# Rows copied one by one on two queues instead of one, and basis products chunk by chunk, in a two-layer relational graph kernel

## The chip, the cores and the metric

The kernel runs on one core of one Trainium2 chip. The metric is device time in microseconds, from the first to the last instruction and what lies around them, for one execution; lower is better. The engines of the core are named as in the profile: PE (matrix products, with PEld for its weight loads), DVE (vector), ACT (scalar), POOL (GpSimd), and SP or SyncE, which computes nothing and issues DMAs. SPq and ACTq mark the instruction queues of SyncE and ACT when they issue DMAs.

## The reference

Two layers of a relational graph convolution over 50,000 nodes of 128 features, a residual, and a layer norm. The edge list holds 800,000 edges and 50,000 self loops, sorted by destination; each edge has one of 16 relations, and the weight of a relation is a mix of 8 basis matrices.

```python
def _rgcn_layer(h, src, dst, rel, basis, w_comp, loop_w, bias):
    W = jnp.einsum('rb,bio->rio', w_comp, basis)
    seg = dst.astype(jnp.int32) * N_REL + rel.astype(jnp.int32)
    agg = jax.ops.segment_sum(h[src], seg, num_segments=N_ENT * N_REL)
    agg = agg.reshape(N_ENT, N_REL, -1)
    msg = jnp.einsum('nri,rio->no', agg, W)
    out = msg + h @ loop_w + bias
    return jax.nn.relu(out)

h = _rgcn_layer(entity_emb, src, dst, rel_type, basis1, w_comp1, loop_w1, bias1)
h = _rgcn_layer(h, src, dst, rel_type, basis2, w_comp2, loop_w2, bias2)

x = _layernorm(x + h, axis=-1)
```

## The kernel before

The edges that are not self loops are cut into tiles of 128 edges (P) and chunks of 10 tiles (K). There are 625 chunks (C), and each of the two layers goes through all of them, so the main loop (L978) makes 1,250 turns. The first turns of the first layer also sort the edge list into its tables (`runs`, `rows_of`), in steps between the other work.

For one chunk the following happens.

- The source rows of its tiles are brought in. A tile is usually one gather on POOL: `gather` (L206) takes 128 indices from `src` and fetches 128 rows of 512 bytes into one of five buffers `g` (GATHERS). The gathers of chunk c + 2 are issued at the start of chunk c (L985 to L988).
- In every eighth chunk the last tile is not gathered. `row_by_row` (L839) copies it: SyncE loads the 128 byte offsets of the tile from DRAM (`row_at`, L842), then, 32 at a time, into its registers (L851, a TENSOR_LOAD in the profile, four for a tile), and for each row issues one DMA of 512 bytes whose source address comes from a register (L859, a MOVE and a DMA_DIRECT2D in the profile). `by_hand` (L835) says which chunks have such a tile: 15, 23, ... 623, which are 77 tiles in a layer. The copy begins BY_HAND + EARLY = 11 chunks ahead of its use and is spread over 8 chunks, one step after each tile of the main loop (L1032).
- DVE builds the weighted one-hot matrix `hot` of a later chunk (`hot_of`, L904), from relation weights that PE makes for four chunks at a time (`weights`, L621). These need the table `rel`, which SyncE loads (L625), and the comparison `is_rel` on DVE (L632).
- PE multiplies each tile's rows by `hot` into the bank `pa` (L1016), five tiles to a bank, and ACT evicts the bank into `aT` (L1024). There are two banks `pa`.
- The sums of four chunks (BATCH) stand side by side in one `aT`, 480 columns. `slots_of_batch` (L750) multiplies them by the 8 basis matrices, 8 products over 480 columns (L754), has ACT copy the result to `by_slot` (L760), transposes it back in four pieces on PE (L764), and `spread_out` (L738) spreads each piece over the places of its nodes on DVE (`slots`, L742). The last five chunks of a layer use `slots` (L728) instead: 8 products of 128 columns for one chunk (L732), whose result needs no transposing.
- `to_nodes` (L785) adds the slots of a chunk into the sums of its group of 512 nodes (`pn`, L796), six chunks behind (LAG). `from_itself` (L681) makes the part of the self loops for a group: it loads `h_own` (L685) and, for every fourth group, the table `lrel` (L652), transposes, and multiplies by the bases (L710, L717, L725). `finish` (L813) closes a group: it adds both parts (L817), and in the first layer applies relu and stores `H1` (L821), in the second adds `x` (`xw`, loaded at L795), normalizes (`normed`) and stores the result (L826).

The order of the work on PE, POOL, DVE and ACT is the order of the program text: `beside` (L952) hands out the steps of the side work between two tiles of the main loop, and the whole loop stands under a manual schedule of these four engines (L898). SyncE isn't in that list; its instructions are placed by the tile framework. Each engine runs its instructions in order, and a DMA that waits for a semaphore holds what is queued behind it. The DMAs that SyncE and ACT issue take their completion semaphores in turn from the same eight (101 to 105 and 107 to 109 in the trace, where ten DMAs of ACT at the start and all of SyncE's use them), and each waits for the DMA that used the semaphore before it.

Of the kernel before, what the change touches and what calls it, by code (L numbers as in the profile page):

```python
# [72 lines left out]
BATCH = 4  # L73
BY_HAND = 8
EARLY = 3
OFFSETS = 32
LAG = BATCH + 2
# [8 lines left out]
def tile_rgcn_resnorm(  # L86
# [33 lines left out]
    assert D == P and N >= P and edges.shape[0] == 1 and AT * NR == P and PER * NB * WN <= BANK and AT * PER * NB == WEIGHTS and PER == HALF and S <= P and C >= 4 and M > 0 and N % C == 0 and N % J == 0 and J * D == BANK and C % BATCH == 1 and C > 4 * BATCH and RUN - LK // 2 == LIVE and C <= RUN and 2 * C <= NG * P and N <= 1 << 16 and E % ROW == 0  # L120
# [10 lines left out]
    ROW_AT = dram.tile([2 * C, P], I32, name="ROW_AT")  # L131
# [310 lines left out]
    def rows_of(j, pool):  # L442
# [36 lines left out]
        row_at = pool.tile([P, LIVE], F32, name="real").bitcast(I32)[:, :P]  # L479
        nc.vector.tensor_scalar(row_at[:m], srcf[:m, LIVE - P :], float(N - 1), float(4 * D), op0=OP.min, op1=OP.mult)  # L480
        nc.sync.dma_start(ROW_AT[r0 : r0 + m], row_at[:m])
# [63 lines left out]
    def count_up(pool):  # L545
        last = 5 * NG + len(ROWS)
        off = pool.tile([P, RUN], F32, name="k_f")[0:1, :C]
        even = pool.tile([P, RUN], F32, name="loop_f")[0:1, :C]
# [48 lines left out]
    def chunked():  # L597
        with (
# [7 lines left out]

            ALONE = C - BATCH - 1

# [12 lines left out]
            def weights(c, n):  # L621
# [9 lines left out]
                is_rel = hp.tile([P, LIVE], F32, name="is_rel", bufs=1)  # L631
# [14 lines left out]
            def loop_weights(g, n):  # L646
# [14 lines left out]
                is_rel = rel.bitcast(F32)  # L661
                for h in range(2):
                    nc.vector.tensor_scalar(is_rel[:m, h, :], rel[:m, h, :], its_rel1[:m], None, op0=OP.is_equal)
                    if h == 0:
                        yield
                po = ps_o.tile([P, BANK], F32, name="po")
                of = po[:, : J * T * NB].rearrange("p (j t) -> p j t", j=J)
                for j in range(J):
                    for h in range(2):
                        nc.tensor.matmul(  # L670
                            of[:, j, :],
                            is_rel[:m, h, :].rearrange("k (p j) -> k p j", j=J)[:, :, j],
                            EACH[n][:m, :T, :].rearrange("k t b -> k (t b)"),
                            start=h == 0,
                            stop=h == 1,
                        )
# [4 lines left out]
            def from_itself(g, of, n):  # L681

                m = nodes(g)
                h = sb.tile([P, J, D], F32, name="h_own", bufs=1)
# [43 lines left out]
            def slots(c, k, aT, n):  # L728

                ps = ps_s.tile([P, BANK], F32, name="ps")  # L730
                for b in range(NB):
                    nc.tensor.matmul(  # L732
                        ps[: k * WN, :D], aT[:, b, : k * WN], BASIS[n][:, b, :], start=b == 0, stop=b == NB - 1
                    )
                    yield
                yield spread_out(c, ps[:, :D])

            def spread_out(c, of):  # L738

                k = ks(c) * WN  # L740
                st = sb.tile([P, J, D], F32, name="slots", bufs=BATCH)
                nc.vector.tensor_tensor(  # L742
                    st[:k],
                    of[:k, None, :].to_broadcast([k, J, D]),
                    which[:k, c, :, None].to_broadcast([k, J, D]),
                    op=OP.mult,
                )
                return st

            def slots_of_batch(c, aT, st, n):  # L750

                ps = ps_s.tile([P, BANK], F32, name="ps")
                for b in range(NB):
                    nc.tensor.matmul(  # L754
                        ps[:, : BATCH * S], BASIS[n][:, b, :], aT[:, b, :], start=b == 0, stop=b == NB - 1
                    )
                    if b < NB - 1:
                        yield
                by_slot = sb.tile([P, BATCH * S], F32, name="by_slot", bufs=1)
                nc.scalar.copy(by_slot, ps[:, : BATCH * S])  # L760
                yield
                po = ps_o.tile([P, BANK], F32, name="po")
                for q in range(BATCH):
                    nc.tensor.transpose(po[:S, q * P : (q + 1) * P], by_slot[:, q * S : (q + 1) * S], ident)  # L764
                    if q == 1:
                        yield
                for q in range(BATCH):
                    st[c + q] = spread_out(c + q, po[:, q * P : (q + 1) * P])
                    if q == 1:
                        yield  # L770
                yield
# [61 lines left out]
            behind = []  # L833

            def by_hand(c):  # L835

                return ks(c) == K and c >= BY_HAND + EARLY and c % BY_HAND == BY_HAND - 1

            def row_by_row(c, of):  # L839

                row_at = hp.tile([1, P], I32, name="row_at")
                nc.sync.dma_start(row_at, ROW_AT[2 * c + 1 : 2 * c + 2])  # L842
                to = hp.tile([P, D], F32, name="by_hand")
                byte = of.bitcast(U8).rearrange("n d -> (n d)")
                yield to
                steps = BY_HAND * (K - 1)
                for step in range(steps):
                    for e in range(step * P // steps, (step + 1) * P // steps):
                        if e % OFFSETS == 0:
                            with tc.issue_after(behind[-1]) if behind else ExitStack():  # L850
                                _, offsets = nc.values_load_multi_w_load_instructions(  # L851
                                    row_at[:, e : e + OFFSETS],
                                    engines=[mybir.EngineType.SP],
# [5 lines left out]
                        behind[:] = [nc.sync.dma_start(row, byte[None, ds(offsets[e % OFFSETS], 4 * D)]).ins]  # L859
# [39 lines left out]
            for n, of in enumerate((x, H1)):  # L899
# [21 lines left out]
                def sum_up(c):  # L921
                    at = c % BATCH * S
                    for st[c] in slots(c, ks(c), aTs[c // BATCH][:, :, at : at + S], n):
                        yield

                def added_in(c):

                    if c < ALONE + 2:
                        return [c - LAG] if c >= LAG else []
                    at = ALONE - BATCH + 2 * (c - ALONE - 2)  # L930
                    return [at, at + 1] if c < C else list(range(at, C))

                def own_of_all():

                    for g in range(NGR):
                        while now[0] < min(first(g) + LAG - 5, C - LAG - 2):
# [9 lines left out]
                def add(c):  # L946

                    for g in to_nodes(c, n):
                        assert made[0] > g
                        ending.append(finish(g, n))  # L950

                def beside(t, c, owning, summing):  # L952
# [3 lines left out]
                    if c < ALONE + 2:  # L956
                        if t in (1, 3, 6, 9):
                            next(summing, None)
                    elif 1 <= t <= 4:
                        for _ in range(NB // 4):  # L960
                            next(summing, None)
                        if t == 4:
                            done(summing)
                            if c == C - 1:
                                done(sum_up(c - 1))
# [3 lines left out]
                    if t == 8:  # L969
                        for one in added_in(c):  # L970
                            add(one)
# [4 lines left out]
                handed, fetching = {}, iter(())  # L976
                owning = own_of_all()
                for c in range(C):  # L978
                    now[0] = c
                    if n == 0 and c:  # L980

                        next(coming, None)
                        while ready[0] + 1 < len(ROWS) and 2 * min(C, c + FETCH + 5 + BY_HAND + EARLY) > ROWS[ready[0] + 1]:
                            next(coming)
                    for to in range(0 if c == 0 else c + FETCH, min(C, c + FETCH + 1)):  # L985
                        buffer = (n * C + to) % GATHERS
                        for k in range(ks(to) - by_hand(to)):
                            gather(rows[buffer][:, k, :], of, src[:, to * K + k : to * K + k + 1])  # L988
                    to = c + BY_HAND + EARLY
                    if to < C and by_hand(to):  # L990
                        fetching = row_by_row(to, of)
                        handed[to] = next(fetching)
                    g = rows[(n * C + c) % GATHERS]
# [7 lines left out]
                    if c % BATCH == 0:  # L1001
                        aTs[c // BATCH] = hp.tile([P, NB, BATCH * S], F32, name="aT")
                    aT, place_of = aTs[c // BATCH], c % BATCH * S
                    if c >= ALONE + 2:
                        if c == ALONE + 2:
                            done(summing)
                        summing = sum_up(c - 2)
                    elif c % BATCH == 0:
                        summing = slots_of_batch(c - BATCH, aTs[c // BATCH - 1], st, n) if c else iter(())
                    for k in range(0, K, PER):  # L1010
# [3 lines left out]
                        for i in range(PER):  # L1014
                            if i < m:
                                nc.tensor.matmul(  # L1016
                                    pa[:, i * NB * WN : (i + 1) * NB * WN],
                                    g[:, k + i, :] if k + i < ks(c) - by_hand(c) else handed.pop(c),
# [4 lines left out]
                            if i == m - 1:  # L1023
                                nc.scalar.copy(  # L1024
                                    aT[:, :, place_of + k * WN : place_of + (k + m) * WN].rearrange(
                                        "d b (i w) -> d i b w", w=WN
                                    ),
# [3 lines left out]
                            if k + i < K - 1:  # L1031
                                next(fetching, None)  # L1032
# [7 lines left out]
                    for one in added_in(c + 1) if c + 1 < C else ():  # L1040
                        masks[one] = masks_of(one)
# [6 lines left out]
                for one in added_in(C):  # L1048
                    masks[one] = masks_of(one)
                    if one == C - 1:  # L1050
                        done(sum_up(one))
                    add(one)
                for each in ending:
# [192 lines left out]
```

## Time and profile before

| what | value |
|---|---|
| median of 3 runs | 18,807.65 us (18,802.19 to 18,828.18) |
| the profiled execution | 18,802.19 us |
| its span, first to last instruction | 18,800.3 us |
| busy: PE / DVE / ACT / POOL | 62% / 36% / 10% / 62% |
| gathers on POOL | 12,346, of 0.946 to 0.949 us each |
| rows copied by SyncE | 19,712, in 154 tiles |
| register loads for them | 616 |
| ACT evictions into aT | 2,500 of 558 ns |
| ACT copies by_slot | 310 of 559 ns |
| mean granted TensorE clock | 0.758 |

A chunk takes 18,800.3 / 1250 = 15.04 us on average. Busy times of the table leave out what an engine spends on issuing DMAs, on registers and on semaphores, so SyncE does not appear in it; its queue is read from the timeline and from the list of what SyncE waits for. "Remote" in a list of waits is a release for which the profile shows no instruction, and "issue" is time in which nothing that the profile shows was waited for.

### The profile page before, as it was taken

The numbers are of one execution on the slowest core, as the hardware profiler recorded it, in microseconds if no ns is written. First come the engines' busy times: TensorE is split into PE (matmuls) and PEld (weight loads), VectorE is DVE, ScalarE is ACT, GpSimd is POOL, SyncE is SP. The second block draws the span as 40 slices with busy tenths as digits, with TensorE's granted clock in tenths as the row PEclk, the third lists the DMA queues.
The fourth block names the chain that finished last, engine by engine and source line by source line (L and its number), as shares of the span: only waits on it lengthen the run. The fifth ranks groups of instructions, "written<-read, shape, count | busy, mean of one in ns | idle before, by whom it ended". The sixth has DMA issues, their size and how long they took to land. (4 is left out here: it accounts for less than half of the span.)

```text
span 18800.3 us, 177030 instructions
## 1 busy us (share of the span) xinstructions
PE 11698.6 (62%) x45072; PEld 7678.2 (41%) x45072; DVE 6710.9 (36%) x11506; ACT 1919.7 (10%) x3706; POOL 11722.7 (62%) x12379
## 2 busy tenths in 40 slices
PE   4565555656566666666656666666666666666666
PEld 3343333434344444444434444444444444444444
DVE  4343434434333333333333333333333333333333
ACT  0000000101000000000001111111111111111111
POOL 5656555665666666666656666666666666666665
PEclk8777777777777777777777777777777777777778
DMA  2222222222111111211112222222222222222221
GB/s 64 62 58 60 56 55 57 58 61 58 54 54 53 53 53 53 54 53 53 53 48 56 56 55 56 56 56 56 56 56 56 56 55 56 56 56 56 56 56 52
DMA packets 576545, 1047.67 MB, mean 56 GB/s; under 512 B 232236, under 2 KB 297674, under 8 KB 575518
## 3 DMA queue, kind: packets, MB, share of 16 engines
q0 software_dynamic: 398624, 816.71, 16.7%
q1 hardware_dynamic: 173678, 218.10, 3.6%
q8 instruction: 366, 6.00, 0.1%
q14 instruction: 661, 5.41, 0.1%
q10 hardware_dynamic: 3216, 1.45, 0.0%
HBM read 962.38 MB, written 72.95 MB: 55 GB/s over the span
## 5 line engine op out<-in xcount | busy, mean ns | idle before, releaser
L206 POOL DMA_INDIRECT g<-H,src x6173 | 5841.2, 946 | 3351.6 <-issue 1363.6
L206 POOL DMA_INDIRECT g<-in_x_dram,src x6173 | 5855.6, 949 | 3273.2 <-issue 1384.3
L1016 PEld LDWEIGHTS pa<-hot,g 128*128 128x128 f32 x24692 | 4644.3, 238 | 5656.9 <-issue 4927.7
L1016 PE MATMUL pa<-hot,g 128*128 128x96 f32 x24692 | 4690.0, 317 | 2628.5 <-issue 2005.6
L754 PE MATMUL ps<-aT,basis 128*128 128x480 f32 x4960 | 2970.5, 684 | 805.0 <-issue 426.6
L1024 ACT COPY aT<-pa 128x480 f32<-128x480 f32 x2500 | 1386.5, 558 | 15442.9 <-remote 8515.6
L796 PE MATMUL pn<-slots,own 120*128 120x512 f32 x4128 | 2523.9, 734 | 665.6 <-DVE slots L742 239.9
L710 PE MATMUL po<-basis,hT 128*128 128x512 f32 x3136 | 2093.6, 756 | 1140.6 <-DVE by L717 774.2
L717 DVE TENSOR_TENSOR by<-po,lw 128x512 f32<-128x512 f32 x1568 | 1066.9, 686 | 4103.6 <-remote 1913.1
L913 DVE TENSOR_TENSOR hot<-fixed,own 128x960 f32<-128x960 f32 x1250 | 1446.5, 1157 | 1582.5 <-remote 708.5
L725 DVE TENSOR_REDUCE ls<-by 128x128 f32<-128x1152 f32 (+1 forms) x784 | 1662.8, 2121 | 35.3 <-DVE by L717 0.9
L742 DVE TENSOR_TENSOR slots<-po,which 120x512 f32<-120x512 f32 x1240 | 780.9, 680 | 2377.2 <-remote 1013.7
L796 PEld LDWEIGHTS pn<-slots,own 120*128 120x128 f32 x4128 | 855.8, 235 | 1237.3 <-issue 729.3
L764 PE MATMUL po<-ident,by_slot 128*120 128x128 f32 x1240 | 374.8, 402 | 1413.2 <-ACT by_slot L760 867.6
L754 PEld LDWEIGHTS ps<-aT,basis 128*128 128x128 f32 x4960 | 898.3, 225 | 862.0 <-issue 471.2
L710 PEld LDWEIGHTS po<-basis,hT 128*128 128x128 f32 x3136 | 578.2, 230 | 1221.6 <-DVE by L717 821.7
L906 DVE TENSOR_TENSOR own<-fixed,key 128x120 bf16<-128x120 f32 x1250 | 343.1, 274 | 1997.9 <-remote 1037.8
L764 PEld LDWEIGHTS po<-ident,by_slot 128*120 128x120 f32 x1240 | 206.0, 208 | 1465.0 <-ACT by_slot L760 911.5
L779 DVE TENSOR_SCALAR own<-col,node 120x128 f32<-120x128 f32 x2064 | 533.7, 297 | 10.4 <-PE pn L796 10.4
L632 DVE TENSOR_SCALAR is_rel<-rel,its_rel 128x640 f32<-128x640 uint8 x314 | 178.5, 568 | 913.8 <-DMA rel<-REL 755.4
L637 PE MATMUL fixed<-each,is_rel 128*128 128x64 f32 x3140 | 445.1, 295 | 6.0 <-DVE is_rel L632 5.7
L637 PEld LDWEIGHTS fixed<-each,is_rel 128*128 128x128 f32 x3140 | 431.7, 216 | 7.1 <-DVE is_rel L632 6.9
(140 smaller groups left out, 3096.2 us busy)
## 6 DMA issues: line engine op xcount, KB each, us to landing
by_hand<-in_x_dram SPq DMA_DIRECT2D x9856, 0.5 KB
by_hand<-H SPq DMA_DIRECT2D x9856, 0.5 KB
g<-in_x_dram,src POOLq DMA_INDIRECT x6173
g<-H,src POOLq DMA_INDIRECT x6173
rel<-REL SPq DMA_DIRECT2D x312, 80.0 KB
h_own<-in_x_dram SPq DMA_DIRECT2D x97, 256.0 KB
xw<-in_x_dram SPq DMA_DIRECT2D x97, 256.0 KB
H<-ls SPq DMA_DIRECT2D x97, 256.0 KB
```

Of the source, the lines that this page charges most:

```text
L206: return nc.gpsimd.indirect_dma_start(out=to, out_offset=None, in_=of, in_offset=bass.IndirectOffsetOnAxis(ap=idx, axis=0))
L637: nc.tensor.matmul(of[:, :, j * NB : (j + 1) * NB], is_rel[:m, j * P : (j + 1) * P], EACH[n][:m], start=True, stop=True,)
L710: nc.tensor.matmul(hb[:m], hT[:, j, :m], BASIS[n][:, b : b + few, :].rearrange("p b d -> p (b d)"), start=True, stop=True,)
L717: nc.vector.tensor_tensor(by[:m, b : b + few, :], hb[:m].rearrange("p (b d) -> p b d", d=D), lw[:m, j, g % T, b : b + few, None].to_broadc ...
L725: nc.vector.tensor_reduce(ls[:m, j, :], by[:m].rearrange("p b d -> p d b"), AX.X, OP.add)
L742: nc.vector.tensor_tensor(st[:k], of[:k, None, :].to_broadcast([k, J, D]), which[:k, c, :, None].to_broadcast([k, J, D]), op=OP.mult,)
L754: nc.tensor.matmul(ps[:, : BATCH * S], BASIS[n][:, b, :], aT[:, b, :], start=b == 0, stop=b == NB - 1)
L764: nc.tensor.transpose(po[:S, q * P : (q + 1) * P], by_slot[:, q * S : (q + 1) * S], ident)
L796: nc.tensor.matmul(sums[g], own, of[:k].rearrange("s j d -> s (j d)"), start=c == first(g), stop=c == final(g),)
L913: nc.vector.tensor_tensor(hot[:, : ks(c)], pm[:, c % Q * K : c % Q * K + ks(c), :, None].to_broadcast([P, ks(c), NB, WN]), own[:, : ks(c), ...
L1016: nc.tensor.matmul(pa[:, i * NB * WN : (i + 1) * NB * WN], g[:, k + i, :] if k + i < ks(c) - by_hand(c) else handed.pop(c), hot[:, k + i]. ...
L1024: nc.scalar.copy(aT[:, :, place_of + k * WN : place_of + (k + m) * WN].rearrange("d b (i w) -> d i b w", w=WN), pa[:, : m * NB * WN].rearr ...
```

## The change

- The basis products are made for each chunk. `slots_of_batch` and `spread_out` go; `slots` serves all chunks, two chunks behind, and DVE spreads its result from the bank `ps` directly. The copy `by_slot` on ACT and the four transposes go too. A chunk is added to its nodes three chunks behind instead of six.
- Two engines copy rows. HANDS names them: SyncE takes the last free tile of the chunks c > 5 with c % 5 = 4 (9, 14, ... 624), ACT that of the chunks c > 6 with c % 6 = 2 (8, 14, ... 620). These are 124 and 103 tiles in a layer. Where a chunk has both, SyncE takes the last tile and ACT the one before it. ROW_AT holds two tiles of offsets for a row of edges instead of one; the offsets of both engines are loaded by SyncE. A copy begins one chunk more than its period ahead of use (6 and 7 chunks), and is spread over 5 and 6 chunks.
- Some buffers become separate or more: `is_l` for the compared `lrel`, two each for `h_own` and `is_rel`, three `aT` of one chunk.

```diff
-BATCH = 4
-BY_HAND = 8
-EARLY = 3
+SP_EVERY = 5
+ACT_EVERY = 6
...
-    ROW_AT = dram.tile([2 * C, P], I32, name="ROW_AT")
+    ROW_AT = dram.tile([2 * C, 2, P], I32, name="ROW_AT")
...
-                is_rel = hp.tile([P, LIVE], F32, name="is_rel", bufs=1)
+                is_rel = hp.tile([P, LIVE], F32, name="is_rel")
...
-                is_rel = rel.bitcast(F32)
+                is_rel = hp.tile([P // 2, 2, P, J], F32, name="is_l", bufs=1)
...
-                h = sb.tile([P, J, D], F32, name="h_own", bufs=1)
+                h = sb.tile([P, J, D], F32, name="h_own", bufs=2)
...
-                yield spread_out(c, ps[:, :D])
-
-            def spread_out(c, of):
-
-                k = ks(c) * WN
-                st = sb.tile([P, J, D], F32, name="slots", bufs=BATCH)
+                st = sb.tile([P, J, D], F32, name="slots")
                 nc.vector.tensor_tensor(
-                    st[:k],
-                    of[:k, None, :].to_broadcast([k, J, D]),
-                    which[:k, c, :, None].to_broadcast([k, J, D]),
+                    st[: k * WN],
+                    ps[: k * WN, None, :D].to_broadcast([k * WN, J, D]),
+                    which[: k * WN, c, :, None].to_broadcast([k * WN, J, D]),
                     op=OP.mult,
                 )
-                return st
-
-            def slots_of_batch(c, aT, st, n):
-
-                ps = ps_s.tile([P, BANK], F32, name="ps")
-                for b in range(NB):
-                    nc.tensor.matmul(
-                        ps[:, : BATCH * S], BASIS[n][:, b, :], aT[:, b, :], start=b == 0, stop=b == NB - 1
-                    )
...
-                by_slot = sb.tile([P, BATCH * S], F32, name="by_slot", bufs=1)
-                nc.scalar.copy(by_slot, ps[:, : BATCH * S])
...
-                    nc.tensor.transpose(po[:S, q * P : (q + 1) * P], by_slot[:, q * S : (q + 1) * S], ident)
...
+                yield st
...
-            behind = []
+            behind = {}
+            HANDS = ((nc.sync, SP_EVERY, SP_EVERY - 1), (nc.scalar, ACT_EVERY, ACT_EVERY // 2 - 1))

             def by_hand(c):

-                return ks(c) == K and c >= BY_HAND + EARLY and c % BY_HAND == BY_HAND - 1
-
-            def row_by_row(c, of):
-
-                row_at = hp.tile([1, P], I32, name="row_at")
-                nc.sync.dma_start(row_at, ROW_AT[2 * c + 1 : 2 * c + 2])
-                to = hp.tile([P, D], F32, name="by_hand")
+                if ks(c) < K:
+                    return []
+                return [i for i, (_, every, at) in enumerate(HANDS) if c > every and c % every == at]
+
+            def row_by_row(i, c, of):
+
+                engine, every, _ = HANDS[i]
+                tile_at = 1 - by_hand(c).index(i)
+                row_at = hp.tile([1, P], I32, name=f"row_at{i}", bufs=2)
+                nc.sync.dma_start(row_at, ROW_AT[2 * c + 1 : 2 * c + 2, tile_at])
+                to = hp.tile([P, D], F32, name=f"by_hand{i}", bufs=2)
                 byte = of.bitcast(U8).rearrange("n d -> (n d)")
                 yield to
-                steps = BY_HAND * (K - 1)
+                steps = every * (K - 1)
                 for step in range(steps):
                     for e in range(step * P // steps, (step + 1) * P // steps):
                         if e % OFFSETS == 0:
-                            with tc.issue_after(behind[-1]) if behind else ExitStack():
+                            with tc.issue_after(behind[i]) if i in behind else ExitStack():
                                 _, offsets = nc.values_load_multi_w_load_instructions(
                                     row_at[:, e : e + OFFSETS],
-                                    engines=[mybir.EngineType.SP],
+                                    engines=[engine.engine],
...
-                        behind[:] = [nc.sync.dma_start(row, byte[None, ds(offsets[e % OFFSETS], 4 * D)]).ins]
+                        behind[i] = engine.dma_start(row, byte[None, ds(offsets[e % OFFSETS], 4 * D)]).ins
                     yield to
...
-                        for k in range(ks(to) - by_hand(to)):
+                        for k in range(ks(to) - len(by_hand(to))):
                             gather(rows[buffer][:, k, :], of, src[:, to * K + k : to * K + k + 1])
-                    to = c + BY_HAND + EARLY
-                    if to < C and by_hand(to):
-                        fetching = row_by_row(to, of)
-                        handed[to] = next(fetching)
+                    for i, (_, every, _) in enumerate(HANDS):
+                        to = c + every + 1
+                        if to < C and i in by_hand(to):
+                            fetching[i] = row_by_row(i, to, of)
+                            handed.setdefault(to, {})[K - 1 - by_hand(to).index(i)] = next(fetching[i])
...
-                    elif c % BATCH == 0:
-                        summing = slots_of_batch(c - BATCH, aTs[c // BATCH - 1], st, n) if c else iter(())
+                    aT = aTs[c] = hp.tile([P, NB, S], F32, name="aT", bufs=3)
+                    summing = sum_up(c - 2) if c > 1 else iter(())
```

## The prediction, made before the changed kernel was run

> **What bounds the kernel now.** I first read the page: which engine is fullest, and what it does. Then the list of waits, the SyncE queue's own waits, and the timelines of the SyncE queue and of POOL, side by side.
>
> ```profile
> PE 11698.6 (62%) x45072; PEld 7678.2 (41%) x45072; DVE 6710.9 (36%) x11506; ACT 1919.7 (10%) x3706; POOL 11722.7 (62%) x12379
> ...
> L206 POOL DMA_INDIRECT g<-H,src x6173 | 5841.2, 946 | 3351.6 <-issue 1363.6
> ...
> by_hand<-H SPq DMA_DIRECT2D x9856, 0.5 KB
> ```
>
> No engine is full. POOL issues 12,346 gathers of 128 rows (6,173 per layer), 0.946 us each; its timeline shows how close they can stand:
>
> ```profile
> 14532.79 0.94 POOL L206 DMA_INDIRECT g<-H,src  x1 [0.30 <-issue]
> 14534.03 0.94 POOL L206 DMA_INDIRECT g<-H,src  x1 [0.30 <-issue]
> ```
>
> One gather every 1.25 us at best (14534.03 - 14532.79, rounded up), so POOL needs 12,346 x 1.25 = 15.4 ms of the 18.8 ms. The other 3.4 ms are waits. The list of waits says for what, and the queue's own list what SyncE (SPq) waits for (us in total, times, longest):
>
> ```profile
> POOL g L206 <- PE pa L1016: 1382.1, 1649, 7.8
> PEld po L764 <- ACT by_slot L760: 911.5, 143, 15.7
> DVE is_rel L632 <- DMA rel<-REL: 755.4, 77, 29.4
> DVE lrel L663 <- DMA lrel<-LREL: 389.1, 47, 26.9
> ...
> SPq L821 <- ACT ls L820: 893.7, 59, 105.3
> ```
>
> POOL waits for PE to free a buffer. DVE, in front of PE, waits up to 29 us at a time for two small tables that SyncE loads. Why are the tables late? The SyncE queue over one hand-copied tile, with its register load:
>
> ```profile
> 14525.56 21.90 SPq L859 DMA_DIRECT2D by_hand<-H  x32
> 14547.47 0.00 SPq L625 DMA_DIRECT2D rel<-REL  x1
> 14549.63 6.86 SPq L859 DMA_DIRECT2D by_hand<-H  x16
> 14570.15 0.38 SPq L826 DMA_DIRECT2D out_dram<-ls  x1
> 14570.63 33.60 SPq L859 DMA_DIRECT2D by_hand<-H  x46
> ...
> 14605.06 0.57 SPq L859 DMA_DIRECT2D by_hand<-H  x2
> ...
> 14609.04 20.51 SPq L859 DMA_DIRECT2D by_hand<-H  x32
> ```
>
> ```profile
> L851 SPq TENSOR_LOAD <-row_at x616: 3/2052/4437, 50.3 to 18711.9; - x154
> L859 SPq DMA_DIRECT2D by_hand<-H x9856: 2/224/1430, 9601.5 to 18733.1; - x198
> ```
>
> The 128 rows took 21.90 + 6.86 + 33.60 + 0.57 + 20.51 = 83.4 us, 0.65 us a row, and the four register loads of a tile take about 2.05 us each. The tables (L625) stand in the same queue behind the rows. So SyncE, not an engine of the busy table, paces this kernel. Its account for a chunk (18,800 / 1250 = 15.04 us): 19,712 / 1250 = 15.8 rows x 0.65 = 10.3; 616 x 2.05 / 1250 = 1.0; its other loads and stores about 0.5 (each 0.4 to 0.7 in this stretch); together 11.8. The remaining 3.2 us are waits for results of other engines (L821 is the largest) and gaps.
>
> What sets the price of a row? I looked for stretches of 32 rows with and without gathers beside them, and the windows give POOL's gathers in each (the fifth busy figure):
>
> ```profile
> 1366.71 10.28 SPq L859 DMA_DIRECT2D by_hand<-in_x_dram  x32
> ...
> 2389.80 47.59 SPq L859 DMA_DIRECT2D by_hand<-in_x_dram  x32
> ```
>
> ```profile
> 1366.00:1378.00 12.00, 10.04 (x29) 5.79 (x30) 11.45 (x21) 1.12 (x2) 0.00 (x0) 0.66 0.01 3
> 2389.00:2438.00 49.00, 13.54 (x70) 9.31 (x68) 4.11 (x8) 1.68 (x3) 37.11 (x40) 0.66 0.24 67
> 14500.00:14620.00 120.00, 81.13 (x304) 53.32 (x305) 40.38 (x72) 13.20 (x26) 75.47 (x80) 0.74 0.22 60
> ```
>
> A row costs 10.28 / 32 = 0.32 us with no gather beside it, 0.65 at 80 / 120 = 0.67 gathers per us, and 47.59 / 32 = 1.49 at 40 / 49 = 0.82. Rows on the hardware queue get dearer the denser POOL gathers. I use the straight line through the first two: r = 0.324 + 0.49 x (gathers per us).
>
> **The change part by part.**
>
> *Rows on SyncE.* One tile in 5 chunks: chunks 9, 14, ... 624 are 124 tiles a layer, where 77 were. That is 248 x 128 = 31,744 rows, 25.4 a chunk, where 15.8 were. At today's 0.65 us they alone take 16.5 us of a chunk that lasts 15.04. Register loads: 248 x 4 x 2.05 / 1250 = 1.6 us. Other loads 0.5, and ACT's index rows (206 loads of about 0.2 us) hardly count.
>
> *Rows on ACT.* Chunks 8, 14, ... 620: 103 tiles a layer, 26,368 rows, 21.1 a chunk. No row of this trace prices them. Ends: 0.32 us (SyncE without gathers) and 1.49 (SyncE under dense ones). I take SyncE's r at the same density, the nearest row. At 0.52 gathers per us that is 0.58: 12.2 us, plus 206 x 4 x 2.05 / 1250 = 1.35 us of register loads, plus ACT's own work, 1919.7 us less the removed copies (310 x 0.559 = 173), 1.4 us a chunk: 15.0 us. So ACT, 10% busy now, becomes nearly full. Behind each row in its order stand the evictions at L1024 that PE needs, and behind its register load, which waits for an index row that SyncE must have loaded, stands everything else.
>
> *Gathers.* 2 x (124 + 103 - 77) = 300 fewer, 12,046, or 9.64 a chunk: 300 x 1.25 = 375 us less for POOL, which is worth its price only if POOL sets the end.
>
> *Bases for each chunk.* PE loses eight matmuls over 480 columns and four transposes in four chunks, and gets eight small products a chunk. Today's tail has such products:
>
> ```profile
> 18774.04 1.98 PE L732 MATMUL ps<-basis,aT 128*120 128x128 f32 x16 [0.88 <-DVE slots L742]
> ```
>
> That is 1.98 us for the eight products of a chunk. In the same tail's timeline one product over 480 columns holds PE for 0.83 us before the next matmul starts, and the four transposes of L764 for 0.66 us: (8 x 0.83 + 0.66) / 4 = 1.83 us a chunk. So PE gets 0.15 us more a chunk; the cover is PE's idle 38%, and without it this costs 0.15 x 1250 = 190 us. I take nothing. The ACT copy by_slot goes, and with it PE's wait of 911.5 us: a gain between 0 and 912 us. I take 0, because PE then waits for the next late table or tile. DVE's products keep count and shape; they only read another bank. The separate buffers (is_l, h_own, hot, is_rel) let loads start earlier, but these loads stand in the SyncE queue, so they gain nothing while it is behind: 0.
>
> *The sum.* SyncE needs, for a chunk of T us: 25.4 x (0.324 + 0.49 x 9.64 / T) + 1.6 + 0.5 = 10.3 + 120 / T. With no waits T = 10.3 + 120 / T gives 17.3 us (21.6 ms); with all of today's 3.2 us of waits and gaps, 19.6 us (24.5 ms). Waits should shrink when the queue is always late, but there is a second row engine to be late for: I take 1.9 us: T = 12.2 + 120 / T gives 18.6 us, x 1250 = 23,300 us (**23,300**). The profiled execution took 18,802.2 us, its span 18,800.3; the median of the runs is 5.5 us above, which doesn't matter here.
>
> The Trainium skill has two rules here. The row of the first: issuing a row holds SyncE for 0.32 to 1.49 us. DMA: Bandwidth & Descriptors, section Issuing engines are not separate DMA queues, says that issuing from several engines saves only issue time, which is usually small beside the DMA; this trace differs in the second half, since issue time is the whole cost. By the rule's "small" nothing is bound by rows, and the sum would be 18.4 ms. The row of the second: 224 ns is the median of the issue itself. Perfetto Trace Analysis, section DMA Instruction — HWDGE (DVE, Sync), says that the two issuing sequencers share one descriptor generator, locked for a DMA at a time; this speaks against the change. With 46.5 rows a chunk it would be held 46.5 x 0.224 = 10.4 us, which fits, so by it alone the time would not move; no row here shows two sequencers at once.
>
> **The rivals.**
>
> *A, POOL sets the end and rows fit.* Then 18,802 - 375 = 18,430 us, or down to 17.5 ms with the 912 us. For: SyncE does issue rows at 0.32 us. It holds while 25.4 r + 2.1 stays below 18,430 / 1250 = 14.7 us, so r below 0.50 us at 0.65 gathers per us. Against: the tile above paid 0.65 there. Near its edge it is no change.
>
> *B, evictions behind rows.* ACT's order puts about 11 rows between two evictions. If in each half chunk PE's work (11,698.6 / 1250 = 9.4 us a chunk) waits for ACT and ACT for PE, the two add up: about 21.1 x 0.52 + 2.75 + 9.4 = 23.2 us, 29.0 ms. Two buffers (pa) let PE run half a chunk ahead; with half of PE's work hidden T is about 19, like the forecast.
>
> *C, rows of both engines pass one place.* Then 46.5 rows pay in turn: T = 46.5 x (0.324 + 0.49 x 9.64 / T) + 2.1 gives 25.7 us, 32.1 ms. For: gathers and rows already hinder one another. Against: nothing shows that it is a queue.
>
> **How the numbers follow.** Forecast 0.69, with its own range of 21.0 to 25.5 ms; A 0.12; B 0.12; C 0.07. The range goes from A's 18,400 to 27,500 us, where B is partly inside; about 0.15 stays outside. A measurement tells 0.2% from no change: faster 0.10, within 0.2% 0.02, slower 0.88.
>
> **What would show it.** Right: rows on SyncE near 0.55 to 0.65 us with hardly a pause, POOL's busy share down from 62% to about 50%, its waits for PE longer, DVE's waits for rel and lrel longer, ACT full of row issues. Wrong: rows at 0.5 us or less, SyncE waiting for ACT or DVE in each tile, and POOL near 80% by its 1.25 us beat. If ACT's evictions have rows ahead of them and PE waits at pa while SyncE idles, it is B; if rows on both engines are above 0.8 us at a thinner gather stream, C.

## The result, and the profile after

The changed kernel took 22,133 us (median of 4 runs, 22,125 to 22,157), the kernel before 18,809 us in the same comparison: 1.177 times as long, 95% interval 1.175 to 1.179. The prediction was 23,300 us and slower.

The page of the changed kernel (line numbers are those of the new text: L836 is the row copy, L204 the gather, L972 the product into `pa`, L980 its eviction by ACT):

```profile
PE 12179.0 (55%) x58712; PEld 9290.6 (42%) x58712; DVE 6776.9 (31%) x11506; ACT 1789.6 (8%) x3396; POOL 11422.0 (52%) x12079
...
L204 POOL DMA_INDIRECT g<-H,src x6023 | 5693.1, 945 | 5163.9 <-PE pa L972 2829.1
...
L980 ACT COPY aT<-pa 128x480 f32<-128x480 f32 x2500 | 1395.5, 558 | 17984.9 <-DMA by_hand<-H 5420.3
```

Each gather costs what it did, 0.945 to 0.947 us, and there are 300 fewer, but POOL now stands idle for longer before them, mostly for PE. The SyncE queue is the first place to look for the reason. Its timeline over 120 us:

```profile
14500.25 36.37 SPq L836 DMA_DIRECT2D by_hand<-H  x47
14537.09 0.02 SPq L798 DMA_DIRECT2D out_dram<-ls  x1
14537.20 36.40 SPq L836 DMA_DIRECT2D by_hand<-H  x48
14573.67 0.36 SPq L767 DMA_DIRECT2D xw<-in_x_dram  x1
14574.71 42.09 SPq L836 DMA_DIRECT2D by_hand<-H  x80
14616.85 0.63 SPq L623 DMA_DIRECT2D rel<-REL  x1
14617.59 2.61 SPq L836 DMA_DIRECT2D by_hand<-H  x8
```

There is no pause left. The rows (with the register loads between them) fill 36.37 + 36.40 + 42.09 + 2.61 = 117.5 of 120 us; the pause of 13.7 us that stood in the same stretch of the kernel before (from 14549.63 + 6.86 = 14556.49 to the store of L826 at 14570.15) has no counterpart. The list of waits shows who waits (us in total, times, longest), and the second fence the SyncE queue's own waits:

```profile
POOL g L204 <- PE pa L972: 5434.5, 2165, 27.7
ACT aT L980 <- DMA by_hand<-H: 5420.3, 780, 30.6
...
PEld pa L972 <- ACT aT L980: 3410.0, 533, 46.0
...
DVE is_rel L630 <- DMA rel<-REL: 3234.5, 150, 61.8
```

```profile
SPq L836 <- DMA by_hand<-in_x_dram: 694.3, 908, 9.0
SPq L836 <- DMA by_hand<-H: 660.3, 877, 9.6
```

Three lines of the kernel before, to compare with:

```profile
PEld pa L1016 <- ACT aT L1024: 548.0, 117, 37.6
...
SPq L859 <- DMA by_hand<-H: 199.3, 404, 1.4
SPq L859 <- DMA by_hand<-in_x_dram: 187.8, 380, 1.5
```

DVE's wait for the table rel went from 755 to 3,235 us: the table stands behind more rows. PE's wait for ACT's evictions went from 548 to 3,410 us: the evictions stand behind ACT's rows (ACT aT L980 <- DMA by_hand). POOL's wait for PE went from 1,382 to 5,435 us. And SyncE's own waits for row DMAs, 387 us and at most 1.5 us long before, are now 1,355 us and up to 9.6 us long.

Added up over the whole trace, the SyncE queue spends 18.81 ms on the rows (31,744 MOVEs and DMAs with the gaps before them) and 2.01 ms on 992 register loads; with its other loads, stores and waits that is the whole 22.16 ms. From one row to the next it takes 0.586 us on average, where it took 0.725 in the kernel before.

### The profile page after: what moved, and what is told of

Its sections match the earlier page's. It is cut to its first block, busy times and chain, and to the rows that moved or that the text cites. A ratio compares the mean times of both kernels' runs of the same rounds, so it can differ in the third digit from the quotient of the medians.

```text
span 22155.5 us, 283113 instructions
## 1 busy us (share of the span) xinstructions
PE 12179.0 (55%) x58712; PEld 9290.6 (42%) x58712; DVE 6776.9 (31%) x11506; ACT 1789.6 (8%) x3396; POOL 11422.0 (52%) x12079
## 3 DMA queue, kind: packets, MB, share of 16 engines
q0 software_dynamic: 389024, 797.03, 13.7%
## 5 line engine op out<-in xcount | busy, mean ns | idle before, releaser
L972 PE MATMUL pa<-hot,g 128*128 128x96 f32 x24092 | 5029.9, 322 | 6128.5 <-ACT aT L980 3300.5
L204 POOL DMA_INDIRECT g<-H,src x6023 | 5693.1, 945 | 5163.9 <-PE pa L972 2829.1
L204 POOL DMA_INDIRECT g<-in_x_dram,src x6023 | 5703.1, 947 | 4988.4 <-PE pa L972 2605.4
L972 PEld LDWEIGHTS pa<-hot,g 128*128 128x128 f32 x24092 | 4554.9, 240 | 7898.9 <-issue 4413.0
L732 PE MATMUL ps<-basis,aT 128*120 128x128 f32 x20000 | 3799.1, 320 | 232.4 <-issue 219.4
L732 PEld LDWEIGHTS ps<-basis,aT 128*120 128x120 f32 x20000 | 3161.5, 222 | 258.9 <-issue 248.8
L768 PE MATMUL pn<-slots,own 120*128 120x512 f32 x4128 | 2725.4, 785 | 981.4 <-DVE own L751 849.6
L737 DVE TENSOR_TENSOR slots<-ps,which 120x512 f32<-120x512 f32 x1250 | 860.5, 688 | 7821.4 <-remote 3051.6
L980 ACT COPY aT<-pa 128x480 f32<-128x480 f32 x2500 | 1395.5, 558 | 17984.9 <-DMA by_hand<-H 5420.3
L670 PE MATMUL po<-each,is_l 64*128 64x32 f32 (+1 forms) x800 | 206.1, 419 | 755.2 <-DVE is_l L661 676.4
L695 PE MATMUL po<-ident,h_own 128*128 128x128 f32 (+1 forms) x784 | 210.5, 363 | 660.3 <-DMA h_own<-H 367.8
L670 PEld LDWEIGHTS po<-each,is_l 64*128 64x128 f32 (+1 forms) x800 | 193.5, 324 | 770.9 <-DVE is_l L661 689.4
```

The source lines that it names most:

```text
L204: return nc.gpsimd.indirect_dma_start(out=to, out_offset=None, in_=of, in_offset=bass.IndirectOffsetOnAxis(ap=idx, axis=0))
L732: nc.tensor.matmul(ps[: k * WN, :D], aT[:, b, : k * WN], BASIS[n][:, b, :], start=b == 0, stop=b == NB - 1)
L737: nc.vector.tensor_tensor(st[: k * WN], ps[: k * WN, None, :D].to_broadcast([k * WN, J, D]), which[: k * WN, c, :, None].to_broadcast([k * ...
L768: nc.tensor.matmul(sums[g], own, of[:k].rearrange("s j d -> s (j d)"), start=c == first(g), stop=c == final(g),)
L972: nc.tensor.matmul(pa[:, i * NB * WN : (i + 1) * NB * WN], others.get(k + i, g[:, k + i, :]), hot[:, k + i].rearrange("e b w -> e (b w)"), ...
L980: nc.scalar.copy(aT[:, :, k * WN : (k + m) * WN].rearrange("d b (i w) -> d i b w", w=WN), pa[:, : m * NB * WN].rearrange("d (i b w) -> d i ...
```

## The experiments

The first experiments showed something that no one trace could: the kernel before does not take 18.8 ms everywhere. The experiments ran on several chips, and each was compared with the kernel before on its own chip.

| chip | kernel before, us | kernels run there |
|---|---|---|
| of the result above | 18,809 | the changed kernel 22,133 |
| 10 | 15,609 | e1 15,494; e2 15,547; e3 15,801; e4 15,606 |
| 13 | 18,615 | e5 21,912; e6 18,614 |
| 8 | 18,624 | e7 18,541; e9 19,195 |
| 9 | 15,610 | e10 15,498; e11 15,802 |
| 8, later | 18,795 | e13 22,125; e14 20,732 |

So there are two kinds of chip here: 9 and 10, where the kernel before takes 15.6 ms, and 8, 13 and that of the result above, with 18.6 to 18.8 ms. I call them the first and the second kind. The changed kernel, e7 and e11 ran four times each; e1 to e4, e6, e9, e10 and e14 ran once.

**e1, e2, e3: the changed kernel with rows on SyncE alone, on ACT alone, and on neither.** The edits:

```diff
-            HANDS = ((nc.sync, SP_EVERY, SP_EVERY - 1), (nc.scalar, ACT_EVERY, ACT_EVERY // 2 - 1))
+            HANDS = ((nc.sync, SP_EVERY, SP_EVERY - 1),)
...
+            HANDS = ((nc.scalar, ACT_EVERY, ACT_EVERY // 2 - 1),)
...
+            HANDS = ()
```

> The changed kernel without ACT's row tiles (they are gathered again): 248 tiles on SyncE, 12,252 gathers. Theory S (SyncE's queue sets the time; T = 10.3 + 122 / T with 9.80 gathers a chunk): about as the changed kernel, 21.6 to 22.6 ms. Rival E (ACT's evictions wait behind ACT's rows): well under it, 19 to 20.5 ms.

> The changed kernel without SyncE's row tiles: 206 tiles on ACT, 12,294 gathers. S: SyncE has hardly anything to do, the tables come early, and the time falls far below the changed kernel's, to 17 to 19.5 ms. E: ACT's rows still stand before the evictions: 20.5 to 22.5 ms.

> The changed kernel with every tile gathered: no row DMAs, no register loads, 12,500 gathers. S: nothing stands before the tables, POOL keeps its beat of 1.25 us a gather, 15.6 ms, with start and ends 15.8 to 16.8 ms, faster than both kernels. Rival (PE, DVE and ACT waiting on each other): 17.5 to 18.8 ms, since these waits stay.

**e4: only the products for each chunk**, with the rows of the kernel before (one more line, not shown, lets the tables run ahead by the same lead).

```diff
-            HANDS = ((nc.sync, SP_EVERY, SP_EVERY - 1), (nc.scalar, ACT_EVERY, ACT_EVERY // 2 - 1))
+            HANDS = ((nc.sync, SP_EVERY, SP_EVERY - 1),)
...
-SP_EVERY = 5
+SP_EVERY = 8
...
-                return [i for i, (_, every, at) in enumerate(HANDS) if c > every and c % every == at]
+                return [i for i, (_, every, at) in enumerate(HANDS) if c >= every + 3 and c % every == at]
...
-                        to = c + every + 1
+                        to = c + every + 3
```

> The changed kernel with the rows of the kernel before: one tile in 8 chunks on SyncE, none on ACT, a lead of 11 chunks; only the products for each chunk and the separate buffers are left of the change. S: the time of before within 2%, 18.4 to 19.1 ms. Rival (the removed copy by_slot and PE's wait of 912 us were on the path): 17.7 to 18.1 ms. Rival (the products for each chunk cost): over 19.2 ms.

Measured on chip 10: 15,494, 15,547, 15,801 and 15,606 us, and 15,609 for the kernel before. None of the expected contrasts appeared: e1, e2 and e4 lie far below every range named for them, and e3 lies at the low end of S's range, but beside a kernel before that takes 15.6 ms here. All five stand in one line with their gathers: 12,252, 12,294, 12,500, 12,346 and 12,346; from 12,252 to 12,500 the time grows by 307 us, 1.24 us a gather. POOL sets the time on this chip, and the rest is hidden. For e4 and the kernel before (equal counts of gathers, 3 us apart) this says that the products for each chunk cost and bring nothing here.

Why does SyncE keep up here with 25.4 rows a chunk? A stretch of its queue in e1, and the window around it (POOL's gathers are the fifth busy figure):

```profile
12026.72 19.09 SPq L836 DMA_DIRECT2D by_hand<-H  x51
```

```profile
12000.00:12070.00 70.00, 51.88 (x275) 36.94 (x274) 32.03 (x53) 8.91 (x18) 52.91 (x57) 0.94 0.23 62
```

51 rows and one register load of 2.1 us in 19.09 us are 0.33 us a row, beside 57 gathers in 70 us, 0.81 per us. On the prediction's chip a stretch with gathers as dense had cost 1.49 us a row. Over the whole of e1 a row takes 0.335 us; instructions of 0.67 to 0.74 us on the SyncE queue, 6,698 in the trace of before, are 5 here. So gathers alone don't make a row dear: beside them it is dear on the chip of the prediction and cheap on this one.

**e5, e6: the changed kernel and the kernel before once more, unchanged**, to see both on one chip with its traces.

> The changed kernel itself once more, beside the kernel before on the same chip, since the runs so far had the kernel before at 15.6 ms where it took 18.8 ms when the prediction was scored. Theory S (what a row costs SyncE decides): on a chip where a row costs about 0.34 us SyncE needs 25.4 x 0.34 + 2.1 = 10.7 us a chunk, less than POOL's 9.64 x 1.25 = 12.05, so POOL sets the time: 15.2 to 15.4 ms, faster than before by 1.5 to 2.5%; where a row costs 0.58 us with gathers beside it, 22.1 ms again. Rival E (ACT's rows before the evictions cost whatever a row costs): slower than before on such a chip too, 15.8 ms or more.

> The kernel before, for its trace on this chip. S: where it takes 15.6 ms, its rows cost 0.32 to 0.36 us beside gathers at the full beat, and instructions of 0.70 us on the SyncE queue (6,698 in the trace of before) are nearly gone. Rival (the chip differs in the clock of PE, granted at 0.83 to 0.86 instead of 0.76, and this is what made it faster): rows cost as before and the waits for late tables stay.

They ran on chip 13, of the second kind: 21,912 us against 18,615, ratio 1.177 (1.175 to 1.179), the ratio of the first result, with 6,634 instructions of about 0.70 us on the SyncE queue of e6. So the result repeats on another chip of that kind.

**e7, e9: e3 and e2 again.**

> The kernel of e3 (every tile gathered) again, for a chip on which the kernel before takes about 18.7 ms; on the chip of e3 it took 15.6. Theory S (where gathers make rows dear, SyncE's queue sets the time, and nothing else is slower there): 15.7 to 16.0 ms here too, 15% below before. Rival (everything there is slower, by the clock of PE or otherwise): 18 ms or more. If before takes 15.6 ms here, it repeats e3, 15.8 ms.

> The kernel of e2 (rows on ACT alone, 21.1 a chunk) again, for a chip on which before takes about 18.7 ms. S, with SyncE's price of a row taken for ACT: 21.1 x (0.324 + 0.49 x 9.84 / T) + 2.75 = T gives 16.0 us a chunk, 20.0 ms, when ACT never waits; waits for PE's banks come on top, up to 21.5. If ACT pays less for a row than SyncE (its rows in the changed kernel were 0.32 to 0.33 us for more than half of them): 17 to 19 ms. Rival (ACT's rows are what made the changed kernel slow, SyncE's only full beside it): 21.9 ms as the changed kernel.

Both ran on chip 8, of the second kind. e9 took 19,195 us, 3% over the kernel before: under the 20.0 to 21.5 ms of S, over the 17 to 19 ms named for cheaper rows, and ACT's rows alone don't make the 22 ms. e7 took 18,541 us, 0.996 of the kernel before (0.994 to 0.997), where theory S wanted 15.8. This is the miss that matters. With no row on any queue, 98% of SyncE's time is free, and the kernel is as slow as before on that chip. So without any row something else holds the kernel at 18.5 ms there. (e7 also makes the products chunk by chunk, and neither e4 nor e11 ran on such a chip: that these products cost there just what the missing rows gain is not excluded.) The same kernel on the two kinds of chip; first the list of waits of e3 (chip 10):

```profile
PEld pa L972 <- DMA g<-H,src: 2350.1, 3109, 2.8
PEld pa L972 <- DMA g<-in_x_dram,src: 2256.0, 3024, 4.7
...
POOL g L204 <- issue: 1598.7, 5246, 0.3
...
PEld pa L972 <- issue: 866.1, 2393, 25.3
```

then that of e7 (chip 8):

```profile
PEld pa L972 <- issue: 4515.6, 6378, 31.1
POOL g L204 <- issue: 2760.6, 8886, 3.9
PE pa L972 <- issue: 2744.7, 1534, 30.8
POOL g L204 <- remote: 1456.7, 970, 6.8
POOL g L204 <- PE pa L972: 1337.7, 1733, 6.7
```

On chip 10 PE waits mostly for the next gather, which is what a kernel at POOL's beat looks like, and no wait of POOL is longer than 0.3 us in the row shown. On chip 8 PE's longest waits, up to 31 us, are for nothing that the profile shows, and they add up to five times as much as on chip 10 (4,516 us against 866). One such moment in e7, in the timelines of PE, DVE and ACT:

```profile
14513.87 1.17 PE L972 MATMUL pa<-hot,g 128*128 128x96 f32 x4 [9.58 <-issue]
...
14513.26 0.69 DVE L737 TENSOR_TENSOR slots<-ps,which 120x512 f32<-120x512 f32 x1 [11.04 <-remote]
...
14513.26 1.02 ACT L980 COPY aT<-pa 128x480 f32<-128x480 f32 x2 [12.05 <-remote]
```

PE's last matmul before it ended at about 14504.3. DVE and ACT, which wait for PE, go on at the same instant nine microseconds later, and PE after them. In the trace PE's semaphore steps in between stand 0.71, 2.13, 2.10, 2.80 and 1.38 us apart, nearly multiples of 0.70. This is not one moment alone. Over the whole of e7, 2,575, 2,965 and 1,069 of the steps of PE's semaphore are 0.67 to 0.74, 1.36 to 1.44 and 2.06 to 2.16 us long (once, twice and three times 0.70); in e3 529, 210 and 62 are. So on this chip the slowing is not SyncE's alone. Two other readings have the traces against them. DMAs are hardly slower there: a 4 KB packet of a gather takes 0.236 us at the median in e7 and 0.225 in e3. And PE's lower clock does not show in its work: PE is busy for 12.23 ms in e7 and for 12.43 ms in e3.

**e10, e11: rows on SyncE alone again, and the kernel before with no rows.** For e11:

```diff
-                return ks(c) == K and c >= BY_HAND + EARLY and c % BY_HAND == BY_HAND - 1
+                return False
```

> The kernel of e1 (rows on SyncE alone, 25.4 a chunk; 229,171 instructions) again, for a chip on which before takes about 18.7 ms. Theory S (SyncE's queue, 25.4 rows a chunk dear beside gathers, sets the changed kernel's time): 21 to 22 ms, as the changed kernel, for SyncE's work is the same. Theory R, formed after e7 (on such chips every sequencer is slowed in steps of 0.70 us, and the time grows with all that is issued on all engines): between e9 (217,951 instructions, 19.2 ms) and the changed kernel (283,113, 21.9 ms), 19.4 to 20.2 ms, with SyncE waiting for others again. If before takes 15.6 ms here, it repeats e1, 15.5 ms.

> The kernel before with every tile gathered: products in batches of four, no row DMAs, no register loads, some 137,000 instructions, the fewest of all. R: on a chip with before at 18.7 ms it takes less than e7 (163,788 instructions, 18.5 ms), 17.6 to 18.4 ms. Rival (there the waits of PE, DVE and ACT on each other set the time whatever is issued): 18.5 ms or more, as e7, or longer by PE's wait for by_slot. On a chip with before at 15.6 ms: POOL's beat, 15.8 ms, for 154 gathers more.

They ran on chip 9, of the first kind, and tell nothing of the second: 15,498 us, as e1, and 15,802 us (1.012 of before, 1.011 to 1.014), as e3, both as expected for such a chip. They only confirm the beat of POOL, again without a difference between batches and single chunks.

**e13, e14: the changed kernel and rows on SyncE alone, on one chip**, so that one of them would tell something on either kind.

> The changed kernel, with e14 on the same chip. If before takes 15.6 ms there: POOL's beat sets the time, 12,046 x 1.249 = 15.05 ms and the 0.19 ms that e1 to e3 had around their gathers, 15.2 to 15.3 ms, 2 to 2.5% faster than before. Rival E (ACT's rows before the evictions hold PE whatever the chip): over 15.6 ms. If before takes 18.7 ms: 21.9 ms, as before.

> The kernel of e1 and e10 (rows on SyncE alone). If before takes about 18.7 ms there: theory S (SyncE's queue, 25.4 rows a chunk, sets the changed kernel's time) 21 to 22 ms; theory R (the slowing grows with what all engines issue, 229,171 instructions against 217,951 in e9 and 283,113 in the changed kernel) 19.4 to 20.2 ms. If before takes 15.6 ms: 15.5 ms, as e1 and e10.

They ran on chip 8: 22,125 us (1.177 of before, 1.175 to 1.179) and 20,732 us. e14 is between the theories, nearer to S: R's highest was 20.2, S's lowest 21. Its SyncE queue is as full as the changed kernel's (17.68 ms of rows and 1.97 of register loads in 20.73; after the two waits shown, for rows, the next has 54 us in total):

```profile
SPq L836 <- DMA by_hand<-in_x_dram: 274.2, 563, 1.5
SPq L836 <- DMA by_hand<-H: 268.6, 579, 1.4
```

With e7 and e9 the runs on chip 8 make a square: 18,541 us without rows, 19,195 with ACT's, 20,732 with SyncE's, 22,125 with both. The kernel before stood at 18,624 beside the first two and at 18,795 beside the last two, so some 0.17 ms of the differences between the pairs is the chip's. The rows, then, are what makes the changed kernel slower there, and SyncE's cost the most: about 2 ms, by a queue that is full. Theory R, by the number of instructions, does not fit: e14 has 11,220 more than e9 and takes 1.5 ms longer. ACT's rows add 0.65 ms alone and 1,393 us beside SyncE's (22,125 - 20,732). Where do they add the 1,393 us? SyncE's time on rows goes from 17.68 to 18.81 ms (1.13 ms, by the trace of e13), and its waits on semaphores before rows by 0.25 ms: together the difference. In e14 the waits shown are at most 1.5 us long; in the changed kernel such waits reach 9.6. I sorted the gaps of more than 1 us before a row DMA on SyncE by who had last used its semaphore: SyncE itself, 65 gaps and 0.11 ms; ACT, 433 gaps and 1.00 ms, though ACT had used it last for only 10,405 of the 31,744 rows. So by this reading 1.0 of the 1.4 ms are waits for a semaphore that ACT's row holds. ACT waits for SyncE in the same way, and longer: before its rows stand 1,581 gaps of more than 1 us, 3.64 ms in all, where SyncE had used the semaphore last, and 77, 0.16 ms, where ACT itself had. This is read from the trace; a kernel with separate semaphores wasn't tried.

## Why the prediction was right or wrong

- **Slower, inside the range:** yes, on the kind of chip on which the kernel before takes 18.8 ms; 22,133 against 23,300 us, below the middle of the forecast's own 21.0 to 25.5 ms.
- **"SyncE needs, for a chunk of T us ... 10.3 + 120 / T":** held. With no waits it gave 17.3 us a chunk; measured are 22,155 / 1250 = 17.7.
- **The price of a row:** 0.324 + 0.49 x 12,046 / 22,155 = 0.590 us was the line's value at the density that came about; 0.586 was measured. That they meet is partly luck. The slope came from one stretch at 0.65 us; over the whole trace of before a row took 0.725 where the line gives 0.646 (0.657 gathers per us), in e14 0.564 where it gives 0.614 (0.591 per us), and the 0.586 hold 0.03 us a row of waits for ACT's semaphores (1.0 ms / 31,744). Against the density averaged over a run, the line is too flat. (Its 0.324 stands for 10.28 / 32 = 0.321; that changes nothing.) As a law the line is of that kind of chip only: on chip 10 a row costs 0.335 us at 0.79 gathers per us.
- **The term that was mis-sized: the waits.** "I take 1.9 us" for a chunk. Waits for DVE and ACT vanished; what came in their place, SyncE's delay by ACT's rows, is 1.4 ms / 1250 = 1.1 us by e13 and e14 (0.8 us of it the waits on semaphores that ACT's rows hold), and lies mostly in the price of a row. Outside the rows SyncE's gaps are 0.68 ms in all, 0.5 us a chunk where 1.9 were forecast, and the result is close to the sum without waits.
- **ACT's rows:** 12.2 us a chunk forecast; 15.4 ms / 1250 = 12.3 measured, with the gaps. This agreement is luck: 3.6 ms of the 15.4 are ACT's waits on semaphores that SyncE had used last, which the forecast did not have; without them a row took ACT about 0.45 us ((15.4 - 3.6) ms / 26,368, an estimate), not 0.58. "Nearly full" was right, and PE's waits for evictions (3,410 us) fit it. Rival B did not decide: 19.2 ms with ACT's rows alone (e9).
- **Rival C, one place for both engines' rows:** not as priced (32.1 ms). A mild form exists, the shared semaphores that the front part describes and that I had not priced: 1.0 ms of SyncE's time and 3.6 ms of ACT's by the gaps above.
- **The fewer gathers and the products for each chunk at 0:** shown at 0 for the products on chips 9 and 10 (e4 and before, e11 and e3). On the second kind of chip e4 wasn't run, so there this stays open. A gather less is worth 1.24 us on the first kind; what it is worth on the second no run shows.
- **"So SyncE, not an engine of the busy table, paces this kernel" (the kernel before):** not borne out. e7 has no rows and takes the same time on such a chip (with the reservation on the products made above), and in the trace of before SyncE itself waits for ACT and DVE, 894 us at L821 alone. I took late tables, which are real, for the cause of the 3.4 ms; without the rows something else holds the kernel at 18.5 ms. The account of 11.8 us a chunk was low, too: over the whole trace rows (14.09 ms), register loads (1.22) and the other instructions (0.68) make 12.8 us, 85% of the span. The sum for the changed kernel held all the same, because adding 60% of rows to a queue that was already 85% full made it the longest.
- **Rival A, POOL at its beat:** it is what the first kind of chip does. By it the changed kernel would take 15,801 - 454 x 1.249 = 15,234 us there, 2.4% less than before. That is an estimate from e3 and POOL's beat: the changed kernel ran on no chip of that kind.

By DMA: Bandwidth & Descriptors, section Issuing engines are not separate DMA queues, in the Trainium skill, a second issuing engine only saves the time to issue. Here that time was the cost, 0.33 us a row in e1 and 0.59 in the changed kernel, and the second engine made the first one's rows dearer (0.564 us in e14, 0.586 with ACT beside it).

Open stays what the steps of 0.70 us are, why they come with the gathers, and what sets the time of e7 on chip 8. No version was better than before everywhere: no rows at all (e7) is 0.4% faster on chip 8, and 1.2% slower on the first kind; rows on SyncE alone are 0.7% faster on the first kind (two single runs) and 10% slower on chip 8.

## What to carry to other kernels

Work that is moved off a full engine onto queues that no busy table shows has to be priced by those queues' own timelines: here 9.6 more small DMAs a chunk on SyncE made a queue with some 2 us to spare (15% of 15.04) the bound. A late load is a symptom: before calling its queue the bound, take the queue's work away and see whether the time falls. And a price read on one chip may be that chip's; where two engines issue DMAs in turn from a shared set of semaphores, each can also wait for the other.

## What was not expected of the hardware

- The same kernel takes 15.61 ms on two chips and 18.6 to 18.8 ms on the others; rows on SyncE alone and rows on ACT alone differ by 1.54 ms on chip 8 (e14, e9; the kernel before moved by 0.17 ms between the two) and by 0.05 ms on chip 10 (e1, e2), the other way round. The mean granted clock of PE differs too (0.83 to 0.86 against 0.73 to 0.77), yet one gather takes 0.945 to 0.950 us and one ACT eviction 0.56 us on both.
- On the second kind many instructions of the SyncE queue, and PE's signals, move in steps of 0.70 us while gathers are issued: 0.32 us a row with none beside it, 1.49 at 0.82 gathers per us. Over the whole trace of before, 1.4% of the row instructions take 0.67 to 0.74 us where no gather started in the 4 us before their end, 23% where three did, and 55% where four did. ACT's queue has fewer such steps (1,141 in 52,748 instructions of the changed kernel, SyncE's 5,656 in 64,956).
- A register load of 32 offsets takes 2.03 to 2.23 us at the median, on both queues and both kinds of chip.
